# Graph layer with Strassen products on one core: five landing tiles for gathered rows, scratch copies kept in output rows, one accumulator moved to a rotating PSUM bank

## The chip, the cores and the metric

The kernel runs on one core of a Trainium2 chip. The metric is the device time of one execution in microseconds; the median of three runs is given. A profiled execution, which records every instruction, is a fourth one with its own time.

## The reference

Inputs are 1250 nodes with 1024 features, 20000 edges sorted by target, and a type from 0 to 7 for each edge. What is computed, cut to what matters:

```python
h = jnp.maximum(_layernorm(x), 0.0)
def _rgcn(x, edge_index, edge_type, weight, root, bias):
    msgs = x[src]
    out = x @ root + bias
    for r in range(8):
        mask = (edge_type == r).astype(x.dtype)
        sums = segment_sum(msgs * mask[:, None], dst, n)
        cnt = segment_sum(mask, dst, n)
        out = out + (sums / maximum(cnt, 1.0)[:, None]) @ weight[r]
    return out
u = _rgcn(h, ...)
z = concatenate([u, h], axis=1) @ w_gate + b_gate
out = x + tanh(u) * z + h * (1.0 - z)
```

All of it is in float32. There are eleven 1250 x 1024 x 1024 products: one for each of eight edge types, one with `root`, and two with the halves of `w_gate`.

## The kernel before

**Products first, then sums over edges.** The kernel turns the order round: it computes y = h @ weight[r] for all nodes, writes the rows of y to memory, and then collects, for each target node, the rows that its edges name. For each block of 128 targets and each edge "slot" k, GpSimd (POOL) issues an indirect DMA that gathers 128 rows of 4 KB into a landing tile `got` (L1293), and VectorE (DVE) adds the tile, times a weight, to an accumulator `u` (L1298). This pair is called a slot below. There are `GOT` = 4 landing tiles, used in rotation, so the gather of slot k can start only when slot k-4 has been added.

**Stages and products.** The stages s = 0 to 10 are the eleven weight matrices: s = 0 to 7 the types, s = 8 `root`, s = 9 the lower half of `w_gate`, s = 10 the upper half, which needs u. In each stage the node blocks are taken in five pairs, i = 0 to 4 (blocks i and i+5); one pair is one call of `product`. Each product is a Strassen-Winograd scheme: seven half-size products in place of eight, each of four matmul steps of 128 x 128 by 512 columns. They are named by their left factor: p1 (A11), p5 (S1 T1), then S2 T2, p3 (S4 B22), p7 (S3 T3), p2 (A12 B21) and A22 T4. Pairs i = 0 with 1, and 2 with 3, are coupled: three of their seven half products are replaced by second-level schemes over both pairs together (classes `Second`, from stage 1 on, and `Third` and `First`, from stage 4 on). Pair i = 4 stands alone and does the plain seven.

**Order of the work.** TensorE (PE), ScalarE (ACT), VectorE, GpSimd and SyncE (SP) each run their own list in the order in which the program was written; nothing is scheduled by a planner. `product` calls `between(j)` after each of its steps, j = 0 to 6, and that is where the slots are put in. `spread` decides how many: each call adds a number that depends on i, `(8, 11, 11, 12, 8)` for i = 0 to 4, and slots are issued in proportion. The first group of slots (types 0 to 4) runs beside stages 5 to 7, the second beside stages 8 and 9.

**The accumulators.** PSUM has eight banks: two `ps_b` that `lead()` takes in turn, four `ps` that `bank()` takes in turn, and the single banks `ps_n` and `ps_q`. In a product, p5 puts S1 T1 in a bank c, ACT copies it to the quarter c22 of the output row tile (L463), and p3 then accumulates S4 B22 into the same bank c. For pair i = 4 of the stages after 3, c is `ps_n` (`held("ps_n")`). `ps_n` is also the bank `q.c0` of `Third`, which `hold()` takes at i = 0 and i = 2 and which `last_to` adds to two row tiles at the end of i = 1 and i = 3 (L314 to L316).

**Row tiles.** The output of a product goes to two row tiles t[0] and t[1], of 128 x 1024, from a rotation of four named `row`; SyncE writes them to memory in 512 KB DMAs (L571), two tiles at a product's end or one later. The t[1] of i = 4 is the tile that held one of the rows of i = 2; that row is complete only after `last_to` at the end of i = 3, and is written then. In stage 9, i = 4 uses space in `h_op` in place of row tiles.

**Scratch.** p7 copies its bank by ACT (L428) into a scratch tile `part`, and VectorE adds that to c22 (L429); then A22's product is accumulated in the same bank and copied by ACT into c21, the left half of t[1] (L513). `Third.first` copies two sums (L296, L299) into another `part` tile, which `first_to` reads (L307). `part` has two buffers of 2 KB a partition. `left` of `Second` (L211) makes sums that the first PE group of i = 1 needs.

Of the kernel before, what the change touches and what calls it, by code (L numbers as in the profile page):

```python
# [9 lines left out]
F32 = mybir.dt.float32  # L10
# [9 lines left out]
def tile_rgcn_highway(  # L20
# [35 lines left out]
    P = 128  # L56
# [5 lines left out]
    Q = D // 2  # L62
# [8 lines left out]
    EARLY = 3  # L71
# [5 lines left out]
    NTB = R * ND  # L77
    FAR = 1 << 20
    CG = 4
    GOT = 4  # L80
    UB = 4
    LATE = 4
    IDLE = 12
# [18 lines left out]
    rows = ctx.enter_context(tc.tile_pool(name="rows", bufs=4))  # L102
# [155 lines left out]
    class Third:  # L258
# [28 lines left out]
        def second(self, c):  # L287
            Second.add(self, c[:, :H], self.a12, self.b21)

        def first(self):  # L290
            self.b = psum.tile([P, CG, P], F32, name="ps_q", bufs=1).rearrange(
                "p c k -> p (c k)")[:, :H]
            self.c = bank()[:, :H]
            self.p = rows.tile([P, Q], F32, name="part", bufs=2)
            Second.add(self, self.b, self.a11, self.b11, True)
            nc.scalar.copy(self.p[:, :H], self.b)  # L296
            Second.add(self, self.c, self.s1, self.t1, True)
            Second.add(self, self.b, self.s2, self.t2)
            nc.scalar.copy(self.p[:, H:], self.b)  # L299
# [87 lines left out]
                                                                     aop[:, b])  # L387

    def product(aop, w, to, between=lambda j: None, last=None, pieces=1, whole=True,
                fill=None, second=None, third=None, inner=None, first=None, early=None, own=False):  # L390

        c11, c12 = to[0][:, :Q], to[0][:, Q:]
        c21, c22 = to[1][:, :Q], to[1][:, Q:]
        step = [0]  # L400

        def add(b, i, fresh=False, at=slice(0, Q), ks=range(KQ)):
            for k in ks:
                nc.tensor.matmul(b[:, at], aop[:, i, k, :], w.of[i][:, k, at],  # L404
                                 start=(fresh and k == 0), stop=(k == KQ - 1),
                                 skip_group_check=True)

        def done():
            between(step[0])
            step[0] += 1  # L410

        def filled(name):
            if fill and name in fill and fill[name]():
                done()

        def p3():
            add(c, S4)
            if third:
                third(c)
            else:  # L420
                nc.vector.tensor_add(c12, c12, c)
            done()
            filled("third")

        def p7():
            d = rows.tile([P, Q], F32, name="part", bufs=2)
            add(b, S3)
            nc.scalar.copy(d, b)  # L428
            nc.vector.tensor_add(c22, c22, d)  # L429
            done()  # L430
            filled("seventh")
            return d

        def held(name):

            if not own:
                return bank()
            return psum.tile([P, CG, P], F32, name=name, bufs=1).rearrange("p c k -> p (c k)")

        def p2():  # L440
            a = held("ps_q")
            add(a, A12, True)
            nc.vector.tensor_add(c11, c11, a)
            done()

        def p1():
            if first is None:
                b = lead()
                add(b, A11, True)
            else:  # L450
                b = first.late() if inner.holds else first.to1
            nc.scalar.copy(c11, b)  # L452
            done()
            filled("first")
            return b

        def p5(c=None):
            if c is None:
                c = inner.hold() if inner and inner.holds else held("ps_n")
                add(c, S1, True)  # L460
            else:
                add(c, S1, ks=range(KQ // 2, KQ))
            nc.scalar.copy(c22, c)  # L463
            done()
            filled("fifth")
            return c

        if first and inner.holds and early is None and "first" not in fill:
            c = inner.hold()
            add(c, S1, True, ks=range(KQ // 2))  # L470
            b = p1()
            p5(c)
        elif first and inner.holds:
            c = p5()
            b = p1()
        else:
            b = p1()
            if second:
                second()
                p2()  # L480
            c = p5()
        add(b, S2)
        nc.scalar.copy(c12, b)  # L483
        done()
        filled("sixth")
        if whole and not third:
            p3()
            d = p7()
            if not second:
                p2()  # L490
        else:
            def then():
                inner.then(c)
                done()
                filled("third")

            if early:
                then()
            d = p7()
            if third:  # L500
                last(d, 0)
            if not inner:
                p3()
            elif not early and not inner.holds:
                then()
        if early:
            early()
        if pieces == 1:
            add(b, A22)
            if last:  # L510
                last(b, 0)
            else:
                nc.scalar.copy(c21, b)  # L513
        else:
            for j in reversed(range(pieces)):
                at = slice(j * Q // pieces, (j + 1) * Q // pieces)
                b = bank()
                add(b, A22, True, at)
                last(b[:, at], at.start, d[:, at])
        done()  # L520
        filled("fourth")
# [3 lines left out]
    NM = len(mats)  # L525
    fac = []
# [22 lines left out]
    def step(s, i, between=lambda j: None, second=None):  # L549
# [82 lines left out]
        if two:  # L632
# [16 lines left out]
                if q:  # L649
                    fill["seventh"] = lambda: (q.second(q.c0), True)  # L650
            elif i == 1:
                fill = dict(first=lambda: (e.first(), q and q.first(), 0)[-1],
                            fifth=lambda: (e.sixth(), True),
                            sixth=lambda: (e.seventh(), e.to_first(to), 0)[-1])
                if q:
# [7 lines left out]
            elif i == 2 and q:  # L663
                fill = dict(first=lambda: e.first(),
                            sixth=lambda: (q.second(q.c0), True),
                            seventh=lambda: e.sixth(),
                            fourth=lambda: (e.seventh(), e.to_first(to), True))
            elif i == 2:
                fill = dict(sixth=lambda: e.first(),
                            seventh=lambda: e.sixth(),  # L670
                            third=lambda: (e.seventh(), e.to_first(to), 0)[-1],
                            fourth=lambda: (e.fourth(), True))
            elif q:
                fill = dict(first=lambda: (q.first(), e.fourth(), e.to_second(t[0]),
                                           e.fourth_to_second(t[0]), 0)[-1],
                            sixth=lambda: (e.second(), True),
                            seventh=lambda: (e.second_to_first(to), 0)[-1],
                            third=lambda: (put(i - 1, 0, to), 0)[-1])
            else:
                fill = dict(first=lambda: (e.to_second(t[0]), e.fourth_to_second(t[0]), 0)[-1],  # L680
                            sixth=lambda: (e.second(), True),
                            seventh=lambda: (e.second_to_first(to), put(i - 1, 0, to), 0)[-1])
        product(h_op[i], fac[s], t, between=beside, whole=not two, fill=fill, second=second,
                inner=q, first=waiting_first.get((s, i - i % 2)) if two else None,
                early=early if coming else None, own=s > EARLY and not two)
        for part in range(2):
            if part or not two or i % 2:
                put(i, part, t[part])
# [578 lines left out]
    with ExitStack() as edges_part:  # L1267
# [83 lines left out]
        def spread(e, total, parts):  # L1351

            said = [0, 0]
            parts *= 10

            def between(j):
                said[0] += (8, 11, 11, 12, 8)[at_call[0]]
                while said[1] < min(total, -(-total * said[0] // parts)):
                    next(e, None)
                    said[1] += 1  # L1360
                if said[0] == parts:
                    for _ in e:
                        pass

            return between
# [261 lines left out]
        for i in range(NP):  # L1627
# [49 lines left out]
                    scatter_piece(c0, t[1])  # L1677

            if i < NP - 1:
                product(h_op[i % 2], fac[NM - 1], t, between=beside_u, own=True,  # L1680
                        last=lambda *of: finish(1, *of))
                outs.append((2 * i + 1, t[1]))
            else:
                product(h_op[i % 2], fac[NM - 1], t, between=beside_last, last=finish_last, own=True,
                        pieces=2, second=lambda: None,
                        third=lambda c: finish(0, c, Q, rows.tile([P, Q], F32, name="part",
                                                                  bufs=2)))
# [1 line left out]
_INS = ["x", "src", "dst", "edge_type_8", "L0_gnn_weight", "L0_gnn_root", "L0_gnn_bias",  # L1689
        "L0_gnn_w_gate", "L0_gnn_b_gate"]  # L1690
# [19 lines left out]
```

## Time and profile before

| | |
|---|---|
| time, median of 3 runs | 1356.29 us (1352.90 to 1357.86) |
| profiled execution | 1361.76 us |
| its span, first to last instruction | 1360.0 us |
| mean granted TensorE clock | 0.994 |
| slots: gathers issued, and adds of 1282 ns | 193 each |
| mean DMA rate | 199 GB/s |

The profile page gives busy time by engine, the groups of instructions and the chain of work that ended last. Other views of the same execution are the table of waits (who waited for whom, with total, count and longest), the timeline (instructions in order of time, with idle time before each in brackets), and windows (busy time, DMA share and rate in chosen stretches). Instructions are given by engine, line, operation and tiles written <- read. An idle time is put down to the wait that ended last.

### The profile page before, as it was taken

The numbers are of one execution on the slowest core, as the hardware profiler recorded it, in microseconds if no ns is written. First come the engines' busy times: TensorE is split into PE (matmuls) and PEld (weight loads), VectorE is DVE, ScalarE is ACT, GpSimd is POOL, SyncE is SP. The second block draws the span as 40 slices with busy tenths as digits, with TensorE's granted clock in tenths as the row PEclk, the third lists the DMA queues.
The fourth block names the chain that finished last, engine by engine and source line by source line (L and its number), as shares of the span: only waits on it lengthen the run. The fifth ranks groups of instructions, "written<-read, shape, count | busy, mean of one in ns | idle before, by whom it ended". The sixth has DMA issues, their size and how long they took to land.

```text
span 1360.0 us, 13655 instructions
## 1 busy us (share of the span) xinstructions
PE 1337.5 (98%) x4098; PEld 713.7 (52%) x4098; DVE 993.7 (73%) x2049; ACT 384.0 (28%) x852; POOL 602.3 (44%) x510
## 2 busy tenths in 40 slices
PE   9999999999999999999999999999999899999997
PEld 5444455455445545655665665565466456644443
DVE  7855967786794926535978886987878699767875
ACT  3335566465641112211121221211122112122210
POOL 0001655555562456001464655655255475624631
PEclk9999999999999999999999999999999999999999
DMA  8744775854863251144648769888678956879971
GB/s 316 272 178 150 94 136 148 199 86 117 167 175 89 54 169 39 46 155 136 213 139 312 238 227 344 280 282 290 232 231 291 346 186 206 289 275 272 336 201 58
DMA packets 106911, 271.18 MB, mean 199 GB/s; under 512 B 22692, under 2 KB 24946, under 8 KB 106704
## 3 DMA queue, kind: packets, MB, share of 16 engines
q1 hardware_dynamic: 46640, 120.01, 29.5%
q0 software_dynamic: 44064, 118.28, 27.9%
q10 hardware_dynamic: 16128, 31.98, 7.4%
q8 instruction: 32, 0.52, 0.2%
q14 instruction: 47, 0.39, 0.1%
HBM read 212.71 MB, written 75.66 MB: 212 GB/s over the span
## 4 chain that ended last, share of the span: by engine, by line
PE 81%; issue 7%; DMA 7%; POOL 2%; DVE 2%; ACT 0%; POOLq 0%; DVEq 0%; ACTq 0%
PE ps_b L404 41%; PE ps L404 14%; PE ps L218 10%; PE ps_n L404 7%; DMA got<-y,idx 5%; PE ps_q L404 2%; PE ps_b L218 2%; PE ps_q L218 2%; PE ps_n L218 1%; DVE u L1298 1%; PE ps L370 1%; POOL got L1293 1%; DMA hr_dram<-row 1%; DMA y<-row 1%; POOL out_dram L719 1%
## 5 line engine op out<-in xcount | busy, mean ns | idle before, releaser
L404 PE MATMUL ps_b<-w,h_op 128*128 128x512 f32 x1560 | 702.0, 595 | 1.0 <-ACT row L483 0.8
L404 PEld LDWEIGHTS ps_b<-w,h_op 128*128 128x128 f32 x1560 | 291.6, 190 | 329.4 <-issue 319.3
L1293 POOL DMA_INDIRECT got<-y,idx x193 | 270.1, 1399 | 323.6 <-DVE u L1298 195.3
L1298 DVE SCALAR_TENSOR_TENSOR u<-got,w_of,u 128x1024 f32<-128x1024 f32 (+1 forms) x193 | 246.9, 1282 | 65.1 <-DMA got<-y,idx 63.2
L1109 POOL DMA_INDIRECT table<-row_col,at_i x157 | 175.9, 1120 | 159.3 <-DVE at_i L1105 74.3
L404 PE MATMUL ps<-w,h_op 128*128 128x512 f32 (+1 forms) x496 | 220.1, 587 | 0.0
L404 PEld LDWEIGHTS ps<-w,h_op 128*128 128x128 f32 x496 | 93.2, 190 | 100.7 <-issue 98.3
L404 PE MATMUL ps_n<-w,h_op 128*128 128x512 f32 x272 | 128.9, 615 | 9.7 <-DVE row L314 5.9
L404 PEld LDWEIGHTS ps_n<-w,h_op 128*128 128x128 f32 x272 | 53.0, 196 | 77.2 <-issue 62.1
L428 ACT COPY part<-ps_b 128x512 f32<-128x512 f32 x55 | 32.2, 586 | 208.8 <-PE ps_b L404 205.1
L429 DVE TENSOR_TENSOR row<-row,part 128x512 f32<-128x512 f32 x54 | 37.3, 690 | 66.0 <-ACT part L428 60.7
L513 ACT COPY row<-ps_b 128x512 f32<-128x512 f32 x49 | 28.7, 585 | 197.5 <-PE ps_b L404 181.3
L218 PE MATMUL ps<-w,w 128*128 128x256 f32 x288 | 71.3, 380 | 0.0
L218 PE MATMUL ps<-w,h_op 128*128 128x256 f32 x264 | 68.3, 381 | 0.0
L483 ACT COPY row<-ps_b 128x512 f32<-128x512 f32 x54 | 31.6, 586 | 128.5 <-PE ps_b L404 126.0
L218 PEld LDWEIGHTS ps<-w,w 128*128 128x128 f32 x288 | 54.4, 190 | 20.9 <-issue 14.3
L218 PEld LDWEIGHTS ps<-w,h_op 128*128 128x128 f32 x264 | 49.6, 190 | 24.3 <-issue 19.0
L452 ACT COPY row<-ps_b 128x512 f32<-128x512 f32 x54 | 31.7, 587 | 94.6 <-PE ps_b L404 82.1
L1095 DVE SCALAR_TENSOR_TENSOR junk<-k_bc,key_col,before 128x128 f32<-128x128 int32 x157 | 55.1, 351 | 4.2
L1035 DVE TENSOR_TENSOR seen<-seen,ps_n 128x100 f32<-128x100 f32 x157 | 40.3, 256 | 22.6 <-PE ps_n L1030 13.6
L173 DVE TENSOR_TENSOR w<-w,w 128x2048 f32<-128x2048 f32 (+1 forms) x12 | 25.3, 2112 | 35.3 <-PE ps L404 14.6
L1012 ACT ACTIVATE is_lo<-io,less_lo 128x128 bf16<-128x128 f32 x157 | 50.2, 391 | 0.7 <-DMA xh_dram<-xt 0.7
(241 smaller groups left out, 1500.6 us busy)
## 6 DMA issues: line engine op xcount, KB each, us to landing
y<-row SPq DMA_DIRECT2D x72, 512.0 KB
w<-in_L_gnn_weight_dram ACTq DMA_DIRECT2D x21, 1024.0 KB
w<-in_L_gnn_weight_dram SPq DMA_DIRECT2D x10, 1024.0 KB
k_bc<-keys_dram SPq DMA_DIRECT2D x39, 256.0 KB
l_bc<-los_dram SPq DMA_DIRECT2D x39, 256.0 KB
w<-in_L_gnn_w_gate_dram ACTq DMA_DIRECT2D x6, 1024.0 KB
h_dram<-h_op SPq DMA_DIRECT2D x9, 512.0 KB
u<-in_L_gnn_bias_dram SPq DMA_DIRECT2D x9, 512.0 KB
```

Source lines behind the costliest of these rows:

```text
L218: nc.tensor.matmul(p, a[:, k, :], b[:, k, :], start=(fresh and k == 0), stop=(k == 1), skip_group_check=True)
L404: nc.tensor.matmul(b[:, at], aop[:, i, k, :], w.of[i][:, k, at], start=(fresh and k == 0), stop=(k == KQ - 1), skip_group_check=True)
L428: nc.scalar.copy(d, b)
L429: nc.vector.tensor_add(c22, c22, d)
L452: nc.scalar.copy(c11, b)
L483: nc.scalar.copy(c12, b)
L1012: nc.scalar.activation(is_lo[:, i, :], io, AF.Abs, bias=less_lo[:, c0 + i:c0 + i + 1])
L1035: nc.vector.tensor_add(seen[j][:, i, :], was, p[:, i, :])
L1095: nc.vector.scalar_tensor_tensor(junk, o["k_bc"][:, i, :], key_col[:, c:c + 1], before, op0=OP.is_equal, op1=OP.mult, accum_out=rank[:, c: ...
L1109: ins = nc.gpsimd.indirect_dma_start(out=table[:, :], out_offset=bass.IndirectOffsetOnAxis(ap=at_i[:n, i:i + 1], axis=0), in_=row_col[:n, ...
L1293: nc.gpsimd.indirect_dma_start(out=t[:n], out_offset=None, in_=y[g][:, :], in_offset=bass.IndirectOffsetOnAxis(ap=at[:n, d, k:k + 1], axis=0),
L1298: nc.vector.scalar_tensor_tensor(u[:n], t[:n], w, u[:n], op0=OP.mult, op1=OP.add)
```

## The change

`GOT` becomes 5. The scratch tiles `part` are no longer allocated: p7's copy goes into c21 (the place where A22's product is put later), and `Third.first` gets the left half of t[1] for its two sums. The very last product takes its two scratch halves from the landing tiles. Pair i = 4 of stages 4 to 9 takes a rotating `ps` bank for p5 and p3 in place of `ps_n`, and keeps `ps_q` for p2. The stage-10 products keep both. The shares of `spread` become (10, 8, 13, 11, 8).

```diff
-    GOT = 4
+    GOT = 5
...
-        def first(self):
+        def first(self, p):
...
-            self.p = rows.tile([P, Q], F32, name="part", bufs=2)
+            self.p = p
...
         def p7():
-            d = rows.tile([P, Q], F32, name="part", bufs=2)
+            d = c21 if third is None else aside()
             add(b, S3)
             nc.scalar.copy(d, b)
             nc.vector.tensor_add(c22, c22, d)
...
         def held(name):
-            if not own:
+            if name not in own:
                 return bank()
...
-                fill = dict(first=lambda: (e.first(), q and q.first(), 0)[-1],
+                fill = dict(first=lambda: (e.first(), q and q.first(t[1][:, :Q]), 0)[-1],
...
-                fill = dict(first=lambda: (q.first(), e.fourth(), e.to_second(t[0]),
+                fill = dict(first=lambda: (q.first(t[1][:, :Q]), e.fourth(), e.to_second(t[0]),
...
-                early=early if coming else None, own=s > EARLY and not two)
+                early=early if coming else None, own=("ps_q",) if s > EARLY and not two else ())
...
-                said[0] += (8, 11, 11, 12, 8)[at_call[0]]
+                said[0] += (10, 8, 13, 11, 8)[at_call[0]]
...
-                product(h_op[i % 2], fac[NM - 1], t, between=beside_u, own=True,
+                product(h_op[i % 2], fac[NM - 1], t, between=beside_u,
+                        own=("ps_n", "ps_q"),
...
-                product(h_op[i % 2], fac[NM - 1], t, between=beside_last, last=finish_last, own=True,
+                product(h_op[i % 2], fac[NM - 1], t, between=beside_last, last=finish_last,
+                        own=("ps_n", "ps_q"),
                         pieces=2, second=lambda: None,
-                        third=lambda c: finish(0, c, Q, rows.tile([P, Q], F32, name="part",
-                                                                  bufs=2)))
+                        aside=lambda: got()[:, :Q],
+                        third=lambda c: finish(0, c, Q, got()[:, :Q]))
```

The instruction order of both programs shows what moves. TensorE's, with bank names left out, is the same. VectorE's has the same instructions with slots in other places: in stages 6 to 9 one more slot in i = 0, ahead of `Second.left`, two or three fewer in i = 1, one more in i = 2, and the same eleven or so between the c22 add of i = 2 and `last_to` of i = 3. A `u` tile is stored one slot later, so on POOL and SP a few gathers, stores and row writes change places with their neighbours, and POOL fills one more landing tile with zeros.

More of the change, by code (lines that the diff above doesn't have):

```diff
@@ L389, in product @@
     def product(aop, w, to, between=lambda j: None, last=None, pieces=1, whole=True,
-                fill=None, second=None, third=None, inner=None, first=None, early=None, own=False):
+                fill=None, second=None, third=None, inner=None, first=None, early=None, own=(),
+                aside=None):
         c11, c12 = to[0][:, :Q], to[0][:, Q:]
```

## The prediction

> **What bounds the kernel now.** The page comes first. TensorE is busy nearly throughout, so the question is which microseconds it is not, and who owns them. Next comes the table of waits, for PE and for the engines that it waits on.
>
> ```profile
> span 1360.0 us, 13655 instructions
> PE 1337.5 (98%) x4098; PEld 713.7 (52%) x4098; DVE 993.7 (73%) x2049; ACT 384.0 (28%) x852; POOL 602.3 (44%) x510
> ```
>
> The table of waits (who waited, for whom: us in total, times, longest us):
>
> ```profile
> PE ps_n L404 <- DVE row L314: 5.9, 3, 3.2
> PE ps_n L404 <- ACT row L463: 3.9, 2, 2.7
> ...
> POOL got L1293 <- DVE u L1298: 195.3, 90, 8.2
> DVE u L1298 <- DMA got<-y,idx: 63.2, 43, 4.6
> ACT row L463 <- DMA y<-row: 13.4, 2, 8.8
> ACT row L463 <- DMA hr_dram<-row: 11.1, 1, 11.1
> ```
>
> PE waits on two things, and both concern one PSUM tile, ps_n. The timeline puts all five waits at the start of product i=4 of stages s=7 (954), s=8 (1077) and s=9 (1200). Rows of those three places (start, duration, instruction, count up to the end of the window asked for, idle before it):
>
> ```profile
> 954.28 3.70 PE L404 MATMUL ps_n<-w,h_op 128*128 128x512 f32 x8 [0.30 <-DVE row L314]
> ...
> 963.48 0.59 ACT L463 COPY row<-ps_n 128x512 f32<-128x512 f32 x1 [8.83 <-DMA y<-row]
> 964.12 1.13 PE L404 MATMUL ps_n<-w,h_op 128*128 128x512 f32 x2 [2.70 <-ACT row L463]
> ...
> 1077.42 5.40 PE L404 MATMUL ps_n<-w,h_op 128*128 128x512 f32 x8 [2.41 <-DVE row L314]
> 1082.65 3.60 PE L404 MATMUL ps_b<-w,h_op 128*128 128x512 f32 x8
> 1087.40 1.13 PE L404 MATMUL ps_n<-w,h_op 128*128 128x512 f32 x2 [1.15 <-ACT row L463]
> ...
> 1199.77 4.47 PE L404 MATMUL ps_n<-w,h_op 128*128 128x512 f32 x6 [3.18 <-DVE row L314]
> ```
>
> Eight matmuls take 3.60 us, but 5.40 after the 2.41 us pause: a long pause is followed by half clock and costs 1.80 more. Timeline starts show the same 5.40 after the pauses of 2.70 and 3.18; none follows 1.15. So the stalls are: A (s=7) 0.30+2.70+1.80 = 4.8; B (s=8) 2.41+1.80+1.15 = 5.4; C (s=9) 3.18+1.80 = 5.0. Together 15.1 us is all that this change can reach; the other waits are short or lie before the gathers.
>
> The chain behind each: q.last_to (L314 to L316, VectorE) stands behind slot adds (L1298), which wait for gathers; a gather waits for one of four landing tiles. L314 releases ps_n to S1 T1. It also releases the 512 KB write of the row tile that i=4 reuses (954.26, landed 9.1 us later by the chain; 9.3 at 1077.39). ACT's L463 waits for that landing, and S4 B22 accumulates into the bank that L463 reads. Thus two waits hang on L314, one direct, one through a DMA.
>
> How full the DMA is in the stretch that feeds L314 (last columns: DMA share, GB/s):
>
> ```profile
> 925.00:931.00 6.00, 6.00 (x22) 3.78 (x21) 5.82 (x7) 1.80 (x5) 2.90 (x2) 1.00 0.54 156
> 931.00:940.00 9.00, 9.00 (x28) 4.92 (x27) 6.08 (x11) 1.06 (x3) 6.25 (x6) 1.00 0.90 314
> 940.00:951.20 11.20, 11.20 (x35) 6.36 (x34) 6.68 (x8) 1.76 (x3) 5.33 (x4) 1.00 1.00 340
> 1050.00:1053.00 3.00, 3.00 (x15) 2.64 (x15) 2.86 (x5) 1.82 (x4) 2.69 (x2) 1.00 0.47 90
> 1053.00:1062.00 9.00, 9.00 (x28) 4.75 (x27) 5.30 (x10) 1.54 (x3) 5.18 (x6) 1.00 0.97 353
> ```
>
> **The change part by part.**
>
> *S1 T1 of i=4 in a rotating bank.* PE's order is unchanged; six groups of S1 and six of S4 write ps instead of ps_n. The direct wait on L314 goes. The new bank's previous user is e.c of i=2, long read; each later bank moves on by one, and the two that early() takes now follow q.c and p5's bank of i=3, which VectorE has released some 20 us before. Cost 0; if VectorE were 20 us late, those would be the next waits. At C nothing else is waiting (its rows lie in h_op, without a DMA before L463), so C gives its 5.0. At A and B the S4 wait stays: it merely takes over the time. For B, S4 undisturbed would start at 1087.40-1.15-1.80-2.41 = 1082.0, but L463 ends at 1087.35. With L314 no earlier, this edit alone makes one pause of 5.4 and then half clock: 7.2 against 5.4, a loss of 1.8; at A 0.30+2.70 becomes one 3.0 pause, no gain. Alone: 5.0-1.8 = 3.2 us gained.
>
> *Fifth landing tile.* How much earlier is L314? Call it d. From i=2's c22 add to L314 the instruction order has eleven slot adds at s=7 before and after, so only waits can shrink. In the timeline those waits sum to about 8.2 us (A), 8.8 (B), 7.4 (C). Upper bound: a gather leaves one slot earlier, 24/11 = 2.2 us, and the ring is passed 11/4 = 2.75 times: 6 us. Lower bound by bytes: the DMA runs at 0.90 to 1.00 for the rest of the stretch, so all that is won is one 512 KB gather put into the loose start (0.54, 0.47), 0.52 MB at 340 GB/s = 1.5 us. [...] I take d = 2.5, nearer the byte bound, since the last half is full. One more 970 ns memset comes on POOL behind the first gather, near 635, in a stage where PE waits for nothing: 0. SP and POOL only move row writes and stores by a slot.
>
> With d = 2.5: A keeps 3.0-2.5 = 0.5 without half clock, gain 4.3. B keeps 5.4-2.5 = 2.9 and half clock, 4.7, gain 0.7. C 5.0. Sum 10.0. [...]
>
> *Copies in output rows.* Instruction counts stay. The S3 copy (L428) now stands in c21, so the copy of A22's bank (L513) waits for VectorE's L429. In the timeline L429 ends at least 2.8 us before L513 except twice: 1074.99 against 1071.61, 1195.26 against 1193.20. Behind L513 in ACT's order is L452, at 1075.09 and 1196.63, so it slides 0.5 us at most, and its reader, S2, is 6 us off: 0. If VectorE were 4 us later still, ps_b would hold PE. The first sums (L296, L299) in t[1] wait for the row's old write, issued a product (some 20 us) before and landing in 9: 0. L428 then waits until L307 has read them; closest at s=9, 1187.09 against 1187.17, with 1.8 us more before A22 needs the bank. One more slot add (1.28) lies ahead there, but the 4.6 us gather wait before it shrinks: between 0 and 1.5, taken 0.
>
> *Slots spread 10, 8, 13, 11, 8.* i=1 loses two or three adds of 1.28 us where VectorE is busy 27 of 27.5 us, but PE waits nowhere there: 0. i=0 gets one more ahead of Second.left (L211). PE needs that sum 0.8 to 1.0 us after it is made; idle VectorE time ahead of it covers the rest in s=6, 8 and 9, not in s=7: 1.28-0.76 = 0.5 lost.
>
> *The last product* takes two landing tiles for its scratch; their earlier users ended in i=3: 0.
>
> Sum: 10.0-0.5 = 9.5 us against the profiled execution's own 1361.76 (span 1360.0): 1352.3. The median shown, 1356.29, is 5.5 below it. If that difference lies in these stalls, only 9.7 of 15.1 us are there unprofiled and the gain is 6.1; if not, 9.5. Between them: 8.2, so 1348.
>
> **The rivals.**
> - *All three go* (0.17): the ring, not bytes, limits, d over 5. For: POOL waits 195 us on VectorE for tiles. Against: share 1.00. Gain 10 to 15: about 1343.
> - *The bank alone works* (0.22): d near 0, gain about 3: 1353. For: full DMA.
> - *Slower* (0.14): five gathers lengthen the 512 KB row write that L463 awaits by e, with d = 0. A loses e, B 1.8+e, the same place in s=6, now covered by 0.87 us (L463 ends 843.84, S4 at 844.71), loses e-0.87, and then 1.8; C still gives 5.0. At e = 3 that is 3.0+4.8+3.9-5.0 = 6.7: from there it is slower by over 0.5%; at e = 4, 9.7, about 1364. Against: writes took 7 us at s=6 with similar traffic.
> - *It does nothing* (0.05): L314 late by as much as the slack won; 1356.
>
> **How the numbers follow.** About 0.5% (6.8 us) is what a measurement of this kernel can tell from no change. The likeliest case, d of 1.5 to 4, has 0.42 and gains 6 to 12 by the sum, its own range 1344 to 1351; three quarters of it pass 6.8. Faster: 0.32+0.16+some 0.07 of the bank alone = 0.55. Slower: most of its rival, 0.13. Same: 0.32. The range, 1340 to 1360, runs from the removal of all 15 us to a row write some 2.5 us longer.
>
> **What would show it.** Right: no PE wait on L314 and none of 5.40 us for eight matmuls at i=4 of s=9; DVE's 63.2 us of gather waits down to 40 or so; at s=8 a wait of S4 for ACT of 2 to 4 us left. Wrong: S4 waits at s=7 and 8 longer than 2.7 and 5.4; row writes over 12 us; new PE waits on ps_b or on L211's sums; gather waits unchanged.

## Result and profile after

The changed kernel takes 1347.63 us (median of 7 runs, 1345.66 to 1351.09), the kernel before 1357.86 in the same comparison (7 runs, 1350.71 to 1362.89). The ratio is 0.9924, with a 95% interval of 0.9901 to 0.9947: 10.3 us faster, between 7.2 and 13.4. The profiled execution fell from 1361.76 to 1347.63 us.

The page's first rows, after:

```profile
span 1345.6 us, 13662 instructions
PE 1332.0 (99%) x4098; PEld 712.2 (53%) x4098; DVE 995.7 (74%) x2049; ACT 384.0 (29%) x852; POOL 579.9 (43%) x511
```

The table of waits, after: PE's rows that concern the change, and the two rows of the landing tiles (total, times, longest, in us). Code below the edits moved by one line: L1298 is now L1299, L463 is L464.

```profile
PE ps L405 <- ACT row L464: 1.0, 1, 1.0
...
PE ps L218 <- DVE w L211: 0.3, 2, 0.2
...
POOL got L1294 <- DVE u L1299: 195.8, 77, 6.9
...
DVE u L1299 <- DMA got<-y,idx: 31.1, 22, 3.4
```

No wait on L314 is left. The wait of S4 for ACT's copy of c22 is left once, for 1.0 us. VectorE waits 31.1 us for gathers where it waited 63.2. POOL still waits 196 us for landing tiles, as it did before (195): the tiles still hold the gathers back, but these now run far enough ahead.

The timeline at i=4 of s=8, where the stall of 5.4 us was, and at s=9:

```profile
1069.77 3.60 PE L405 MATMUL ps<-w,h_op 128*128 128x512 f32 x8
1073.20 3.60 PE L405 MATMUL ps_b<-w,h_op 128*128 128x512 f32 x8
1077.15 0.58 ACT L464 COPY row<-ps 128x512 f32<-128x512 f32 x1 [6.60 <-DMA hr_dram<-row]
1077.79 3.70 PE L405 MATMUL ps<-w,h_op 128*128 128x512 f32 x8 [0.99 <-ACT row L464]
...
1187.26 3.60 PE L405 MATMUL ps<-w,h_op 128*128 128x512 f32 x8
1190.69 3.60 PE L405 MATMUL ps_b<-w,h_op 128*128 128x512 f32 x8
```

All groups of eight matmuls at the three places take 3.60 or 3.70 us: with the long pauses, the slow groups went too, and the mean granted clock is 0.998 where it was 0.994. At s=8 the row write is still what ACT waits for, but it was issued early enough for 0.99 us to be all that PE sees.

### The profile page after: what moved, and what is told of

Same layout as the page of the kernel before. It is cut to its first block, busy times and chain, and to the rows that moved or that the text cites. A ratio compares the mean times of both kernels' runs of the same rounds, so it can differ in the third digit from the quotient of the medians.

```text
span 1345.6 us, 13662 instructions
## 1 busy us (share of the span) xinstructions
PE 1332.0 (99%) x4098; PEld 712.2 (53%) x4098; DVE 995.7 (74%) x2049; ACT 384.0 (29%) x852; POOL 579.9 (43%) x511
## 4 chain that ended last, share of the span: by engine, by line
PE 79%; issue 7%; DMA 7%; DVE 4%; POOL 3%; ACT 0%; POOLq 0%; DVEq 0%; ACTq 0%
PE ps_b L405 40%; PE ps L405 17%; PE ps L218 11%; DMA got<-y,idx 5%; PE ps_n L405 3%; PE ps_b L218 2%; PE ps_q L218 2%; PE ps_q L405 1%; DVE u L1299 1%; PE ps_n L218 1%; POOL got L1294 1%; DMA got<-hr_dram,node 1%; PE ps L370 1%; DMA hr_dram<-row 1%; POOL out_dram L720 1%
## 5 line engine op out<-in xcount | busy, mean ns | idle before, releaser
L1294 POOL DMA_INDIRECT got<-y,idx x193 | 246.3, 1276 | 326.4 <-DVE u L1299 195.8
L1299 DVE SCALAR_TENSOR_TENSOR u<-got,w_of,u 128x1024 f32<-128x1024 f32 (+1 forms) x193 | 247.1, 1283 | 33.8 <-DMA got<-y,idx 31.1
L405 PE MATMUL ps<-w,h_op 128*128 128x512 f32 (+1 forms) x592 | 263.4, 588 | 1.0 <-ACT row L464 1.0
L405 PEld LDWEIGHTS ps<-w,h_op 128*128 128x128 f32 x592 | 111.3, 190 | 125.0 <-issue 120.8
L430 DVE TENSOR_TENSOR row<-row 128x512 f32<-128x512 f32 x53 | 36.7, 693 | 72.9 <-ACT row L429 72.7
L429 ACT COPY row<-ps_b 128x512 f32<-128x512 f32 x53 | 31.0, 585 | 197.4 <-PE ps_b L405 193.4
L514 ACT COPY row<-ps_b 128x512 f32<-128x512 f32 x49 | 28.6, 584 | 200.3 <-PE ps_b L405 171.5
L405 PE MATMUL ps_n<-w,h_op 128*128 128x512 f32 x176 | 80.1, 592 | 0.0
L484 ACT COPY row<-ps_b 128x512 f32<-128x512 f32 x54 | 31.6, 586 | 135.9 <-PE ps_b L405 131.1
L218 PEld LDWEIGHTS ps<-w,h_op 128*128 128x128 f32 x264 | 49.6, 190 | 24.3 <-issue 18.7
L453 ACT COPY row<-ps_b 128x512 f32<-128x512 f32 x54 | 31.7, 587 | 90.9 <-PE ps_b L405 82.9
L405 PEld LDWEIGHTS ps_n<-w,h_op 128*128 128x128 f32 x176 | 33.4, 190 | 39.5 <-issue 38.7
L464 ACT COPY row<-ps 128x512 f32<-128x512 f32 x37 | 21.6, 585 | 105.2 <-PE ps L405 92.6
```

What stands on the lines that cost most here:

```text
L218: nc.tensor.matmul(p, a[:, k, :], b[:, k, :], start=(fresh and k == 0), stop=(k == 1), skip_group_check=True)
L1294: nc.gpsimd.indirect_dma_start(out=t[:n], out_offset=None, in_=y[g][:, :], in_offset=bass.IndirectOffsetOnAxis(ap=at[:n, d, k:k + 1], axis=0),
L1299: nc.vector.scalar_tensor_tensor(u[:n], t[:n], w, u[:n], op0=OP.mult, op1=OP.add)
```

## The experiments

How early VectorE's `last_to` comes is the quantity that they share. The table gives, from each kernel's timeline, the end of L314 less the end of the A11 group after which PE is ready for S1 T1. A positive number means that ps_n is not yet free. At s=7 and 8 the row write hangs on L314 too: at s=8 it comes too late for S4 already at -1.53 (a wait of 0.7 us in no_bank), and not at -3.36. Each number of the middle columns is from one profiled execution; each ratio is against executions of before taken in the same comparison.

| kernel | landing tiles | s=7 | s=8 | s=9 | VectorE's waits on gathers, us | ratio to before (95%) |
|---|---|---|---|---|---|---|
| before | 4 | 0.25 | 2.35 | 3.13 | 63.2 | |
| after | 5 | -4.30 | -0.96 | -2.04 | 31.1 | 0.9924 (0.9901 to 0.9947) |
| tiles_alone | 5 | -3.64 | -3.36 | -2.75 | 27.1 | 0.9919 (0.9896 to 0.9942) |
| no_bank | 5 | -5.13 | -1.53 | -1.91 | 30.8 | 0.9910 (0.9885 to 0.9935) |
| no_spread | 5 | -4.96 | -0.34 | -3.44 | 30.2 | 0.9894 (0.9870 to 0.9919) |
| bank_alone | 4 | 1.14 | 2.25 | 2.38 | 60.1 | 0.9984 (0.9968 to 1.0000) |
| spread_alone | 4 | 1.03 | 2.29 | 0.39 | 60.8 | 1.0002 (0.9983 to 1.0021) |
| copies_alone | 4 | 0.30 | 2.32 | 1.53 | 58.3 | 1.0010 (0.9992 to 1.0028) |
| no_tiles | 4 | 1.27 | 1.65 | 2.54 | 64.1 | 0.9991 (0.9971 to 1.0011) |
| three_tiles | 3 | 3.70 | 4.81 | 2.14 | 153 | 1.0555 (1.0519 to 1.0590) |
| five_rows | 4 | -0.39 | 3.40 | 3.86 | 67.2 | 0.9946 (0.9926 to 0.9965) |
| five_rows_ps_n | 4 | -0.31 | 3.33 | 2.53 | 64.5 | 0.9976 (0.9963 to 0.9989) |

**One part alone.** First the rotating bank:

```diff
-                early=early if coming else None, own=s > EARLY and not two)
+                early=early if coming else None, own=("ps_q",) if s > EARLY and not two else ())
```

> Only S1 T1 and S4 B22 of i=4 in a rotating bank; four landing tiles, old scratch, old spread. Theory (the bank removes the direct wait on L314 only): at s=9 no PE wait (5.0 us gone), at s=7 one pause of about 3 us and half clock (4.8, unchanged), at s=8 one pause of about 5.4 and half clock (7.2 in place of 5.4). About 3 us faster. Rival (the bank is what took the stalls away): at most 2 us of PE stall left at the three places, 10 us or more faster.

Its timeline at s=7, 8 and 9:

```profile
962.02 6.75 PE L404 MATMUL ps<-w,h_op 128*128 128x512 f32 x8 [2.76 <-ACT row L463]
...
1085.66 6.38 PE L404 MATMUL ps<-w,h_op 128*128 128x512 f32 x8 [4.53 <-ACT row L463]
...
1197.36 3.60 PE L404 MATMUL ps<-w,h_op 128*128 128x512 f32 x8
```

S1 no longer waits anywhere, s=9 is free, and at s=7 and s=8 the same lateness comes back one step on, at S4, as one longer pause with a longer slow stretch (6.75 and 6.38 in place of 3.60). The stalls are 5.9 and 7.3 us, 13.2 in all where before has 15.1. The ratio gives 2.2 us, between 0 and 4.3; about 3 were expected. The bank by itself mostly moves the wait.

Then five landing tiles, with the scratch copies in output rows that make room for the fifth:

```diff
-    GOT = 4
+    GOT = 5
...
-            d = rows.tile([P, Q], F32, name="part", bufs=2)
+            d = c21 if third is None else aside()
```

> Five landing tiles and the copies in output rows that make room for them; ps_n and the old spread stay. Theory (L314 comes about 2.5 us earlier): at s=7 0.5 us of stall, at s=8 about 4.7, at s=9 0.7, so about 9 us faster, and VectorE's gather waits fall from 63 us to 40 or so. Rival (the DMA is full, a fifth tile brings nothing): the three stalls stay at 15 us, time within 2 us of before. Rival (the ring limits): L314 5 us earlier, no stall above 0.5 us, 14 us faster.

No stall is left at the three places. The ratio gives 11.0 us, between 7.9 and 14.1, as much as the whole change. Against the A11 group, L314 came 3.9, 5.7 and 5.9 us earlier than before, where the theory had 2.5; that is the result that the rival with the limiting ring forecast. `GOT` also enters the count by which slots are spread: in this kernel 11 slot adds in place of 12 stand between the c22 add of i=2 and L314 at s=8 and 9, and one add is 1.3 us of the 5.7 and 5.9.

The shares of the slots alone:

```diff
-                said[0] += (8, 11, 11, 12, 8)[at_call[0]]
+                said[0] += (10, 8, 13, 11, 8)[at_call[0]]
```

> Only the shares of the slots, 10, 8, 13, 11, 8. Theory (as many slots stand ahead of L314 as before): stalls at the three places within 2 us of 15, time within 3 us of before. Rival (moving slots out of i=1 is what made L314 early): stalls under 7 us in sum, 8 us or more faster.

No difference in time. Its profiled execution, at 1353.99 us, has 7.7 us of pauses at the three places, where 13 to 17 of stall were expected: L314 is only 0.39 late at s=9, and none of the five pauses was followed by a slow group (below), which cost 5.4 of the 15.1 before. The median shows nothing of it, and single executions of before lie between 1352 and 1362 us here, so this is put down to the difference between executions.

The scratch copies alone, with four tiles:

> Only the scratch copies in output rows, with four landing tiles, ps_n and the old spread. Theory: covered, stalls at the three places 15 us as before, time within 2 us of before. Rival (the added order between VectorE's reads and ACT's copies costs): new PE waits on ps_b behind ACT, 2 to 5 us slower.

No difference either. No new PE wait on ps_b behind ACT appears (0.8 us in all, as before).

**One part undone.** The changed kernel with `GOT = 4`:

> The changed kernel with four landing tiles: bank, spread and copies stay. Theory (bank and spread alone save only the direct wait at s=9 and turn those at s=7 and 8 into longer ones): 10 to 14 us of stall at s=7 and s=8, none at s=9, gather waits 55 to 63 us, 0 to 5 us faster than before. Rival (bank and spread together do what neither does alone): under 5 us of stall and 8 us faster or more.

It is back at the time of before. The pauses at s=7 and 8, each with a slow group behind it, make 11 us of stall, and at s=9 there is none:

```profile
963.26 5.40 PE L405 MATMUL ps<-w,h_op 128*128 128x512 f32 x8 [3.31 <-ACT row L464]
...
1085.59 5.40 PE L405 MATMUL ps<-w,h_op 128*128 128x512 f32 x8 [4.05 <-ACT row L464]
```

This kernel and the changed one differ in `GOT` alone. With five tiles L314 is 5.6, 2.6 and 4.6 us less late at s=7, 8 and 9, though at s=8 the changed kernel has one slot more ahead of it (12 against 11), and VectorE's waits on gathers fall from 64.1 to 31.1 us. So the fifth tile is what brings L314 forward, and it is needed. With ps_n back for S1 T1:

> The changed kernel with S1 T1 of i=4 back in ps_n: five tiles, copies and spread stay. Theory (with five tiles L314 ends less than 3.4 us after A22, so S1 finds ps_n free): stalls as in the changed kernel, about 1 us at s=8, time within 2 us of it, 9 to 12 us faster than before. Rival (the bank carries part of the gain): waits of S1 on L314 at s=8 or 9 of 1 us and more, 3 us or more slower than the changed kernel.

1347.84 us against 1347.63: with L314 before A11's end, S1 doesn't wait for ps_n, S4 waits 0.7 us for ACT, and the bank is worth nothing that can be measured. With the old shares:

> The changed kernel with the old shares 8, 11, 11, 12, 8: five tiles, copies and bank stay. Theory (the new shares put L314 later at s=8 and 9, lag 2.4 and 1.4 us against 0.0 and 0.6 with the old ones): no stall at s=7, 8 or 9, 1 to 3 us faster than the changed kernel, like tiles_alone. Rival (bank and tiles need the new shares): stalls of 2 us or more come back, slower than the changed kernel.

1345.93 us. The ratio's interval overlaps that of the changed kernel, so a gain of 1 to 3 us isn't shown; a stall of 1.2 us stayed at s=8, which the theory did not expect. The new shares aren't needed. Whether they cost a microsecond is open: in the four kernels with five tiles the end of L314 at s=8 lies anywhere from -3.4 to -0.3.

**The ring or the bytes.** The same as tiles_alone with three tiles:

> As tiles_alone, with three landing tiles in place of five. Theory (the ring of landing tiles paces the slots ahead of L314: 28.4 us for 10 slots on four tiles is 11.4 us a lap, 24.5 us on five is 12.2): a lap of about 11 us on three tiles makes 10 slots last some 37 us, L314 8 us later at each of s=6 to 9; 25 to 40 us slower than before. Rival (bytes pace them: a tile less means one gather of 0.52 MB less in the loose start, 1.5 us): L314 1.5 us later at each place, 4 to 8 us slower.

77 us slower (1435.19 against 1358.35). The byte theory allowed 8. Nor was it the sum expected of the ring, 25 to 40: PE's waits come to 67 us in place of 15, many of them for sums of VectorE that had been in time before, and slow groups follow (the mean granted clock is 0.977). The four longest waits of PE in that kernel:

```profile
PE ps_n L405 <- DVE row L314: 13.6, 4, 4.9
PE ps_q L218 <- DVE inner L279: 11.7, 3, 6.5
PE ps_n L405 <- DVE h_op L386: 8.5, 2, 6.7
PE ps_q L405 <- DVE row L444: 8.0, 1, 8.0
```

The stretch from the c22 add of i=2 to L314 in windows at s=7 and, for two of the kernels, at s=9. The first numbers are the window and its length; the last two columns are DMA share and GB/s. Before:

```profile
925.15:953.55 28.40, 28.40 (x86) 15.88 (x84) 19.97 (x26) 4.54 (x9) 14.48 (x12) 1.00 0.86 285
...
1169.80:1199.04 29.24, 26.79 (x81) 14.82 (x79) 21.57 (x26) 5.12 (x10) 15.73 (x13) 1.00 0.91 304
```

After:

```profile
924.90:948.74 23.84, 23.84 (x75) 13.98 (x74) 20.06 (x25) 3.94 (x8) 15.00 (x12) 1.00 0.77 268
...
1158.99:1184.70 25.71, 25.71 (x79) 14.57 (x79) 21.16 (x26) 4.53 (x9) 16.22 (x13) 1.00 0.99 356
```

The changed kernel with four tiles (no_tiles), and three_tiles:

```profile
924.25:953.67 29.42, 29.42 (x88) 16.45 (x87) 20.06 (x26) 5.08 (x10) 14.17 (x12) 1.00 0.88 284
...
943.65:976.96 33.31, 28.27 (x80) 15.65 (x78) 20.06 (x26) 5.02 (x10) 14.71 (x14) 0.95 0.82 281
```

At s=7, all four kernels have eleven slots in this stretch (the expectation above counts ten; the first one starts while the c22 add is still finishing). VectorE is busy for 20 us in each, and the rest is its waits for gathers: 13.0 us with three tiles, 8.2 before, 9.1 in no_tiles and 3.4 after. One tile is thus worth about 5 us there, in either direction, where the byte theory allows 1.5; and with three tiles VectorE waits longest while the DMA is not full (0.82). So the number of tiles paces the slots. The time of a lap is not constant, though: 33.3 us for eleven slots on three tiles is 9.1 us a lap, 28.4 on four 10.3, 23.8 on five 10.8. The theory took it to be constant, and so had three_tiles' stretch too long by some 4 us at s=7.

After the change the stretch is 4.6 us shorter at a lower share of DMA, and by length times rate it moved 6.4 MB where it had moved 8.1. So L314 had not had to wait for all that the DMA moved in the stretch, though the DMA was full for its last 11 us (share 0.99 from 942.35 to 953.55). At s=9, with twelve slots in both, the stretch after moved 356 GB/s at a share of 0.99 in place of 304 at 0.91. A higher rate at a full share is not shown by this, as the kernel before reached 353 GB/s at 0.97 (1053 to 1062, in the prediction's rows); the engines were kept busy for more of the stretch.

**Where the lateness hurts.** The freed 4 KB a partition can also buy a fifth row tile, so that ACT need not wait for the row write. The edit to the changed kernel, which also gets the old shares back:

```diff
-    GOT = 5
+    GOT = 4
...
-    rows = ctx.enter_context(tc.tile_pool(name="rows", bufs=4))
+    rows = ctx.enter_context(tc.tile_pool(name="rows", bufs=5))
```

> The 4 KB a partition that the scratch copies free go to a fifth row tile in place of a fifth landing tile: four landing tiles, old shares, copies in output rows, bank for S1 T1, rotation of five row tiles. Theory (L314 hurts through two waits alone, ps_n and the row write that ACT's copy of c22 waits for): L314 stays 4 to 6 us behind A22 and the gather waits near 60 us, but PE waits for neither: under 1 us of stall at s=7, 8 and 9, 9 to 12 us faster than before. Rival (the late VectorE list reaches PE by another wait as soon as these two are gone): stalls of 5 us or more under other names, under 6 us faster.

The gather waits stay at 67 us and L314 stays 3.4 and 3.9 us late at s=8 and 9, yet PE doesn't pause there: the two waits named are the whole way from L314 to PE at these places. But one product later, in i=0 of s=9, PE waits for another sum. That VectorE no longer catches up because PE no longer pauses is a likely reason, not tested:

```profile
1092.09 1.88 PE L405 MATMUL ps_n<-w,h_op 128*128 128x512 f32 x4
1097.89 2.08 PE L218 MATMUL ps<-inner,inner 128*128 128x256 f32 x4 [3.92 <-DVE inner L279]
```

The ratio gives 7.3 us, between 4.7 and 10.0: between theory and rival. With ps_n kept:

> As five_rows, with S1 T1 of i=4 back in ps_n. Theory: the direct waits on L314 stay (0.3 at s=7, 2.4 and 3.2 with half clock at s=8 and 9), the waits for the row write go: 7 to 10 us of stall, 3 to 6 us faster than before. Rival (without a row write to wait for, the bank is not needed): under 2 us of stall, as fast as five_rows.

The wait for the row write is gone, the direct waits are 3.38 us at s=8 and 2.59 at s=9, and 3.3 us are gained (1.5 to 5.0), as the theory had it. Both ways from L314 to PE are thus shown apart.

## Why the prediction was right, point by point

- *The place and the most that can be won*: three stalls at i=4 of s=7, 8 and 9, in all 15.1 us. Right. Of them 1.0 is left in the profiled execution, which fell by 14.1.
- *The bank*: 5.0 us at s=9, nothing at s=7, a loss at s=8, 3.2 alone. Right when it is made alone (2.2, between 0 and 4.3). The sum gave it the 5.0 of s=9 for good, though, and this is wrong: the tiles free s=9 as well, and without the bank the changed kernel is as fast.
- *The fifth tile*, d = 2.5. This is the term of the sum that was mis-sized. Measured over the four kernels with five tiles, L314 came 3.9 to 5.4 us earlier at s=7, 2.7 to 5.7 at s=8, 5.0 to 6.6 at s=9. At s=8, 1.0 us of the S4 wait was left in place of 2 to 4. The upper bound of 6, counted in laps of the ring, was nearer than the byte bound of 1.5. The byte bound took all that the full DMA moved in the stretch as bytes that L314 must wait for; the windows at s=7 show that this isn't so, and that a tile more or less is worth about 5 us of gather waits. "All three go" was nearly the case that came.
- *Copies*: 0 predicted, within 2 us of 0 measured. *Shares*: 0.5 us predicted lost at L211, 0.3 us of waits on L211 found, in two places; no gain or loss in time.
- *The slower rival*: row writes longer by 3 us. The write that PE waits for at s=8 was issued at 1068.99 and ACT went on at 1077.15, 8.2 us, where it had been 9.4; at s=7 it was 8.6 and had been 9.2: not longer.
- *From the profile to the median*: the sum against the profiled execution was 9.5, the measured fall 14.1; it was then lowered to 8.2 for the median, and 10.3 were measured. Both fall short mainly by d. That the forecast of 1348 was met within half a microsecond is partly luck: the gain was 2.1 larger than forecast, and the median of before came out at 1357.86, 1.6 above the one that the forecast started from. Lowering it was of the right kind: single executions of before spread over 12 us, those of the four kernels with five tiles over 3 to 7 each. That an execution of before near the median has less stall than the profiled one fits this, but none was profiled.
- *Smaller readings*: eleven slots ahead of L314 at s=7, before and after, is what the traces have. The prediction had VectorE busy 27 of 27.5 us in i=1; the windows of s=7, 8 and 9 have 25.0 to 26.2. 15.1 less 5.5 is 9.6, not 9.7, so that the lower gain is 6.0 in place of 6.1. With e = 4 the slower rival comes to 1366 by its own 9.7 us, not 1364. None of this changes the argument.

## What to carry to other kernels

When an in-order engine waits for prefetched data, count laps as well as bytes: time of one lap of the ring, number of items in the stretch, number of buffers. A DMA share of 0.99 over the last 11 us of the stretch at s=7 did not bound the gain here, because not all that was moved was waited for (6.4 MB after, 8.1 before); a run with one buffer more or less settles it. And follow a late instruction to every wait that hangs on it before removing one of them: freeing the nearest moved the pause to the next at s=7 and 8 (2.76 and 4.53 us in bank_alone), with a slow group behind it (6.75 and 6.38 us in place of 3.60).

## What the hardware showed beyond that

The price of a pause was taken as fixed, 1.80 us. It isn't. That the slow groups are half clock can be read from the granted clock, the third number from the end in a window over the first 3.4 us of the slow group in bank_alone:

```profile
962.10:965.50 3.40, 3.40 (x4) 1.43 (x5) 2.57 (x2) 0.36 (x1) 2.86 (x2) 0.50 0.99 334
```

In the kernel before, the granted clock is 0.50 from 1078.40 to 1081.00 too, inside the group of 5.40 us at s=8.

Timeline rows of spread_alone, and of three_tiles:

```profile
1075.26 3.70 PE L404 MATMUL ps_n<-w,h_op 128*128 128x512 f32 x8 [2.34 <-DVE row L314]
```

```profile
848.10 3.70 PE L405 MATMUL ps_n<-w,h_op 128*128 128x512 f32 x8 [2.82 <-DVE row L314]
...
977.70 6.72 PE L405 MATMUL ps_n<-w,h_op 128*128 128x512 f32 x8 [3.75 <-DVE row L314]
...
1252.22 5.40 PE L405 MATMUL ps_n<-w,h_op 128*128 128x512 f32 x8 [2.19 <-DVE row L314]
```

A pause of 2.34 or 2.82 us passed without slowing, while one of 2.41 in the kernel before and one of 2.19 here cost 1.80, and 3.75 cost 3.12. In the twelve traces the shortest pause with a slow group behind it is 2.02 us and the longest without one 2.82; between them it went either way, and every pause from 3.16 us up had a slow group behind it. What decides it in between was not shown.
